# A fused decoder on one NeuronCore: rotary tables made by products and kept in DRAM, and an earlier timetable for keys and queries

## The chip, the cores and the metric

The kernel runs on one core of a Trainium2 chip. The core has a matrix engine (TensorE, PE in the profile; its weight loads are PEld), a vector engine (VectorE, DVE), a scalar engine with function tables (ScalarE, ACT), a general engine (GpSimd, POOL), and SyncE (SP), which here only issues DMA transfers. Each engine works off its own queue in order, and the engines wait for each other through semaphores. Data lie in DRAM, in SBUF (128 partitions) and in PSUM, where matmuls leave their results. The metric is the device time of one execution in microseconds (us); less is better.

## The reference

The program is a two-layer decoder over four batches of 256 tokens with 256 features. It runs six stages one after the other: rotary self-attention, attention to a masked memory, a ternary feed-forward, a convolution with a recurrence, attention of the tokens to a context of 1601 vectors and to themselves, and a mixture of eight experts of which each token takes two. The change lies in the last two. Cut to these, with the norms that come before them:

```python
x = x + xattn(_layernorm(x), ctx_2048, ...)          # 4 batches, 16 query heads, 4 key heads, 128 wide
x = x + experts(_layernorm(x), ...)

def _rope(x, pos):
    freqs = pos[:, None, :, None] * (1.0 / 10000.0 ** (arange(0, 128, 2) / 128))
    emb = concatenate((freqs, freqs), axis=-1)
    x1, x2 = split(x, 2, axis=-1)
    return x * cos(emb) + concatenate((-x2, x1), axis=-1) * sin(emb)

q = _rope(_rms_norm(tokens @ Wq.T, q_norm_w), token_positions)
kv_in = concatenate([context, tokens], axis=1)       # 1601 + 256 = 1857 keys
k = _rope(_rms_norm(kv_in @ Wk.T, k_norm_w), all_positions)
v = kv_in @ Wv.T                                     # k, v: each head serves four query heads
out = softmax(q @ k.T / sqrt(128)) @ v @ Wo.T

top_logits, top_idx = top_k(xf @ w_gate, 2)
weights = softmax(top_logits)
```

A key or query head of 128 values has two halves of 64. Rotation multiplies both by cosines, and adds the other half times sines. The norm's weights (`q_norm_w`, `k_norm_w`) can be multiplied into the cosines and sines, and the norm's scale, one number for a token or key and head, can be applied later.

## The kernel before

The first four stages of all batches take about the first 505 us. After that comes the part that the change touches: a loop over 32 pairs of query heads (two pairs to each of 16 heads (b, g), batch b and key head g), with the experts of batches 0 to 2 strewn in, until about 1700 us; the last batch's experts end the program.

**One pair** (class `Pair`). The queries of two heads and all 256 tokens are the 512 columns of each score matmul. The 1857 keys, tokens first, are 15 chunks of 128 (NCH); a pair has eight steps of two chunks (the last step has one). A step's `score` does, for each chunk, the matmul bsc (L1361), a copy on ACT that scales by the keys' norm kn (L1362), and on VectorE the running maximum acc (L1364, L1366). After the eighth step `maximum` transposes acc on TensorE (tm, L1373), VectorE reduces (mq, L1375), and TensorE spreads the result over the partitions (bc, L1379, in a PSUM bank of its own). Ten steps after its score, each step's `exponential` subtracts bc (L1383, VectorE), takes the exponential (L1386, ACT), and adds into the softmax's sum on POOL (L1389, L1398; fifteen sums for a pair). Eleven steps after its score, `weigh` multiplies by the values (bpo, L1407). So the second pair of a head scores while the first is weighed. `finish` divides by the sum and multiplies by Wo (bpw, L1437).

**What a head needs before its first score.** `prep_q(b, g, j)` makes the queries of one group of 128 tokens: two matmuls pq (L1239), the rotation (`rotate`: a square on ACT for the norm, L1189, and two products on VectorE with the tables ctab and stab, L1190 and L1191), then `factor`: an addition on POOL (ropeq, L1196), a reduction on VectorE (ssq, L1198), and a power on POOL (rnq, L1199). After a `yield`, ACT scales the four heads by rnq (`normed`, L1203). After another, TensorE transposes them (tpq, L1251) and ACT copies them to qT. `prep_kv(b, g, i)` does the same for unit i of up to four key chunks (pk, L1290); the power gives kn, which the score's copy applies later, and after one `yield` come the transposes tpk (L1301) and the copy to kT (L1303). Context keys and values of the last batch and part of the values of others are projected in advance and kept in DRAM (`kept_keys`, `kept_values`); `prep_kv` loads such raw keys, and `tiles` such values, by DMA on SP.

**Tables.** `angles(b)` makes, a piece at a time, cosines and sines for the 15 chunks' positions. `tables(b)` multiplies them by the norm's weights: four products for the keys (15 x 64 elements a partition each, L1160, L1161, L1164, L1165) and four small ones for the queries. A table has, for each chunk, 128 values in a row: the first half's 64, then the second's.

**The order.** The functions are generators. `steps` runs the loop; each step has two places, and `others(place)` advances the generators that `put` has set down for that place in the dictionary `places`. The timetable is relative to `base`, the place of the head before's first step, so a head's own scores begin at base + 32:

```python
QA, KA, HB, HC = (2, 6), (11, 13, 15, 17), 5, 8      # in steps for QA and KA, in places for HB and HC
DE, DW = 10, 11                                      # exponential and weighing come so many steps after a score
```

So the two query groups start at base + 4 and + 12, are scaled five places later, and transposed eight places after their start; key units 0 to 3 start at base + 22, 26, 30 and 34. A batch's first head also has its tokens' norm (-8, -6, -3), its query tables (-5, -3) and its key tables (+7, +11) there. `experts(b)` of an earlier batch goes in 23 pieces. A scheduler then orders each engine's queue from dependencies, so the order in the queues is not exactly that of the places. PSUM is a ring of six banks shared by all `p1` tiles, one bank for bc and one for the weighing's sum.

**Inverse roots.** `rsqrt` takes one instruction on VectorE and a power on POOL (L266 to 273); `newton` is eleven short ones on VectorE, with no POOL (L275 to 287). The norm ahead of attention (`normed_tokens`) and the one ahead of the experts (`experts`) use `rsqrt`.

**Routing.** In `experts` the two best logits' difference w2 is subtracted on VectorE and ACT's exponential of it (L1026) is issued in the same piece as the two maxima.

Of the kernel before, what the change touches and what calls it, by code (L numbers as in the profile page):

```python
# [20 lines left out]
P = 128  # L21
# [95 lines left out]
def decoder_kernel(ctx: ExitStack, tc: tile.TileContext, at, t, out):  # L117
# [861 lines left out]
    def experts(b):  # L979
# [10 lines left out]
        iota = cc("iota8")[:, None, :].to_broadcast(s8)  # L990
        mv = moments(xb, f"mo{b}")
        yield
        r1 = rsqrt(mv[:, :, 1], 1e-5, f"mo{b}")
        yield
        xh = centred(ea(f"mxh{b}"), xb, mv, r1)
        yield
# [26 lines left out]
            hots.append(oh)  # L1023
        w2 = sm([P, 2], "w2", f"w2{b}", 1)
        V.tensor_sub(w2, tops[1], tops[0])
        A.activation(w2, w2, AF.Exp)  # L1026
        yield
        w1 = sm([P, 2], "w1", f"w1{b}", 1)
# [86 lines left out]
    def angles(b):  # L1115
# [29 lines left out]
        d["angles"] = (ang, sn)  # L1145
        yield

    def tables(b, only="kq"):

        d = bt[b]  # L1150
        ang, sn = d["angles"]
        for nm, n, w in (("k", NCH, knw), ("q", 2, qnw)):
            if nm not in only:
                continue
            tb = [P, n, 64]
            ctab = wk.tile([P, n, HD1], F32, tag=f"c{nm}", name=f"ctab{nm}{b}")
            stab = wk.tile([P, n, HD1], F32, tag=f"s{nm}", name=f"stab{nm}{b}")
            wlo, whi = w[:, None, 0:64].to_broadcast(tb), w[:, None, 64:128].to_broadcast(tb)
            d[nm] = (ctab, stab)
            V.tensor_mul(ctab[:, :, 0:64], ang[:, 0:n, :], wlo)  # L1160
            V.tensor_mul(ctab[:, :, 64:128], ang[:, 0:n, :], whi)  # L1161
            yield

            V.scalar_tensor_tensor(stab[:, :, 64:128], sn[:, 0:n, :], -1.0, whi, ALU.mult, ALU.mult)  # L1164
            V.tensor_mul(stab[:, :, 0:64], sn[:, 0:n, :], wlo)  # L1165
            yield

    def normed_tokens(b):
        mv = moments(xs[b], f"xb{b}")
        r1 = rsqrt(mv[:, :, 1], 1e-5, f"xb{b}")  # L1170
        bt[b]["centred"] = lambda: centred(fa(0, f"bxh{b}"), xs[b], mv, r1)

    def token_features(b):
# [12 lines left out]
    def rotate(src, ctab, stab, sq, r, u):  # L1186


        A.activation(sq[:, :, 0:HD1], src, AF.Square)  # L1189
        V.tensor_mul(r, src, ctab)  # L1190
        V.tensor_mul(u, src, stab)  # L1191

    def factor(sq, r, u, n, nm, rn):

# [10 lines left out]
    def tiles(b, g):  # L1205

        if (b, g) not in gt:
            gt[b, g] = {

                "kT": odd("w3", f"kTb{b}{g}") if g % 2 else wk.tile([P, NKEY], F32, tag="kT", name=f"kTb{b}{g}"),  # L1210
                "v": (
                    odd("w4", f"vb{b}{g}")[:, 0 : NCH * HD1] if g % 2 else wk.tile([P, NCH * HD1], F32, tag="v", name=f"vb{b}{g}")
                ).rearrange("p (c d) -> p c d", c=NCH),
                "kn": sm([P, NCH], f"kn{g % 2}", f"kn{b}{g}", 1),
                "wkv": weight(
                    wk.tile([P, 512], F32, tag="wkv", name=f"wkv{b}{g}", bufs=2), "wkv1", 0, D, g * 256, (g + 1) * 256
                ),
            }
            for i in range(4):
                if (b, i) in kept_values:  # L1220
                    n, w = units(i)
                    r = min(P, w)
                    nc.sync.dma_start(
                        out=gt[b, g]["v"][0:r, 4 * i + 2 : 4 * i + 2 + n, :],
                        in_=kept_values[b, i][:, 0:r, g * HD1 : (g + 1) * HD1].rearrange("c p n -> p c n"),
                    )
        return gt[b, g]

    def prep_q(b, g, j):
        d, e = bt[b], tiles(b, g)  # L1230
        if j == 0:
            e["wq"] = weight(
                fb(0, f"wq{b}{g}"), "wq1", 0, D, g * 512, (g + 1) * 512
            )
            e["qT"] = fb(0, f"qTb{b}{g}").rearrange("p (h t) -> p h t", h=4)
        nm = f"q{b}{g}{j}"
        pq = p1(f"p{nm}")
        for c in range(2):
            T.matmul(pq, lhsT=d["yT"][:, c, j * P : (j + 1) * P], rhs=e["wq"][:, c, :], start=c == 0, stop=c == 1)  # L1239
        ctab, stab = (a[:, j : j + 1, :].to_broadcast([P, 4, HD1]) for a in d["q"])  # L1240

        rn = sm([P, 4], "rn4", f"rn{nm}", 4)
        sq, r, u = rope_tiles(nm)
        rotate(pq.rearrange("p (h d) -> p h d", h=4), ctab, stab, sq, r, u)
        factor(sq, r, u, 4, nm, rn)
        yield
        normed(r, rn, 4)
        yield
        tp = p1(f"tp{nm}")
        for h in range(4):  # L1250
            T.transpose(tp[:, h * P : (h + 1) * P], r[:, h, :], ident)  # L1251
        A.copy(e["qT"][:, :, j * P : (j + 1) * P], tp.rearrange("p (h t) -> p h t", h=4))
# [5 lines left out]
    def prep_kv(b, g, i):  # L1258

        d, e = bt[b], tiles(b, g)  # L1260
        nm = f"k{b}{g}{i}"
        n = min(4, NCH - 4 * i)
        k0 = max(0, 4 * i - 2)
        w = (4 * i + n - 2 - k0) * P
        done = 0
        if b in kept_keys:
            done = n if i else 2
            raw = db(f"raw{nm}")[:, 0 : done * HD1].rearrange("p (c d) -> p c d", c=done)
            nc.sync.dma_start(
                out=raw, in_=kept_keys[b][k0 : k0 + done, :, g * HD1 : (g + 1) * HD1].rearrange("c p n -> p c n")  # L1270
            )
        else:
            cT = db(f"cT{nm}")[:, 0 : 2 * w].rearrange("p (c n) -> p c n", c=2)
            nc.sync.dma_start(out=cT, in_=t["ctxT"][b][:, k0 * P : k0 * P + w].rearrange("(c p) n -> p c n", p=P))
        sq, r, u = rope_tiles(nm)
        if done:
            o = n - done
            ctab, stab = (a[:, 4 * i + o : 4 * i + n, :] for a in d["k"])
            rotate(raw, ctab, stab, *(a[:, o:n, :] for a in (sq, r, u)))
        for h in range(0, n - done, 2):  # L1280
            m = min(2, n - h)
            pk = p1(f"p{nm}{h}").rearrange("p (c n) -> p c n", c=2)
            there = [k >= 2 and (b, (k - 2) // 4) in kept_values for k in range(4 * i + h, 4 * i + h + m)]
            for q in range(m):
                k = 4 * i + h + q
                w = HD1 if there[q] else 2 * HD1
                for c in range(2):
                    o = (k - 2 - k0) * P
                    src = d["yT"][:, c, k * P : (k + 1) * P] if k < 2 else cT[:, c, o : o + P]
                    T.matmul(pk[:, q, 0:w], lhsT=src, rhs=e["wkv"][:, c, 0:w], start=c == 0, stop=c == 1)  # L1290
            ctab, stab = (a[:, 4 * i + h : 4 * i + h + m, :] for a in d["k"])
            rotate(pk[:, 0:m, 0:HD1], ctab, stab, *(a[:, h : h + m, :] for a in (sq, r, u)))
            assert len(set(there)) == 1
            if not there[0]:
                A.copy(e["v"][:, 4 * i + h : 4 * i + h + m, :], pk[:, 0:m, HD1:256])

        factor(sq, r, u, n, nm, e["kn"][:, 4 * i : 4 * i + n])
        yield
        tp = p1(f"tp{nm}")
        for q in range(n):  # L1300
            T.transpose(tp[:, q * P : (q + 1) * P], r[:, q, :], ident)  # L1301
        w = min(512, NKEY - 512 * i)
        A.copy(e["kT"][:, 512 * i : 512 * i + w], tp[:, 0:w])  # L1303

    def before_head(b, g):

        if g == 0:
            if b == 0:
                yield from angles(b)
            yield from tables(b)  # L1310
        late = None
        for i in (1, 2, 3):
            gen = prep_kv(b, g, i)
# [138 lines left out]

    QA, KA, HB, HC = (2, 6), (11, 13, 15, 17), 5, 8
    DE, DW = 10, 11
    places, taken = {}, set()
    STEPS = NPAIR * len(pairs) + DW + 5
# [34 lines left out]
    for k, (b, g) in enumerate(heads):  # L1493
        base = 32 * (k - 1)
        if k:
            if g == 0:
                gen = angles(b)
                for i in range(9):
                    put(base - 81 + 6 * i, gen, i == 8)
                gen = tokens(b)  # L1500
                for i, o in enumerate((-8, -6, -3)):
                    put(base + o, gen, i == 2, i == 2)
                for o, n in ((-5, "q"), (-3, "q"), (7, "k"), (11, "k")):
                    gen = tables(b, n) if o in (-5, 7) else gen
                    put(base + o, gen, o in (-3, 11))
            for f, when in ((prep_q, QA), (prep_kv, KA)):
                for i, o in enumerate(when):
                    gen = f(b, g, i)
                    spot = put(base + 2 * o, gen, bank=f is prep_q)
                    if f is prep_q:  # L1510
                        put(spot + HB, gen)
                    put(spot + HC, gen, True, True)
        gen = loader(b, g)
        put(base + 60, gen, True)
    for b in range(B - 1):
        gen = experts(b)
        spot = 2 * (64 * (b + 1) + 17)

        pieces = 23 if b < B - 2 else 23 - 2 * KEPT
        for i in range(pieces):  # L1520
            spot = put(spot, gen, i == 22, i not in (0, 1, 2, 5, 6)) + (5 if i > 6 else 3)
    kept = gen

    def others(place):
# [145 lines left out]
```

## Time and profile before

| | |
|---|---|
| three runs before | 1749.51, 1746.26, 1751.23 us; median 1749.51 |
| the profiled execution's own time | 1749.43 us |
| its span in the trace | 1747.4 us |
| mean granted TensorE clock | 0.993 |
| instructions in the trace | 20643 |
| DMA traffic | 119.10 MB, mean 68 GB/s |

The page follows the work that ended last back through the program: 64% of the span is on PE, 12% on DVE, 9% each on POOL and ACT, 4% is issue and 1% DMA. Of lines, the weighing bpo (L1407) has 17%, the scores bsc (L1361) 16%, and the key projections pk (L1290) and POOL's sums (L1398) 5% each.

The costliest groups, with their count and the mean time of one:

| engine, line | what | count | mean of one |
|---|---|---|---|
| PE L1361 | scores bsc, 512 columns | 960 | 599 ns |
| PE L1407 | weighing bpo, 512 columns | 960 | 598 ns |
| ACT L1362 | copy of scores | 480 | 683 ns |
| DVE L1366 | running maximum | 448 | 743 ns |
| DVE L1383 | scores less maximum, 2 x 512 | 256 | 1142 ns |
| ACT L1386 | exponential, 2 x 512 | 256 | 1006 ns |
| POOL L1398 | softmax's sum, 512 | 411 | 1306 ns |
| ACT L1203 | scaling of the queries | 128 | 390 ns |

How to read this: a matmul of 128x512 is listed as x4 because the compiler cuts float32 matmuls into four passes; 480 score tiles are thus 960 listed here in two forms (counts in the trace are of instructions as the profiler saw them). The share of busy time is a mean over a program of two very different parts. The first 505 us and the pair loop have other limits, so the stretches of the loop have to be read by themselves. An idle engine costs time only if it is the one that the end waits for; here the question is what PE waits for inside the loop, and for how long.

### The profile page before, as it was taken

The numbers are of one execution on the slowest core, as the hardware profiler recorded it, in microseconds if no ns is written. First come the engines' busy times: TensorE is split into PE (matmuls) and PEld (weight loads), VectorE is DVE, ScalarE is ACT, GpSimd is POOL, SyncE is SP. The second block draws the span as 40 slices with busy tenths as digits, with TensorE's granted clock in tenths as the row PEclk, the third lists the DMA queues.
The fourth block names the chain that finished last, engine by engine and source line by source line (L and its number), as shares of the span: only waits on it lengthen the run. The fifth ranks groups of instructions, "written<-read, shape, count | busy, mean of one in ns | idle before, by whom it ended". The sixth has DMA issues, their size and how long they took to land.

```text
span 1747.4 us, 20643 instructions
## 1 busy us (share of the span) xinstructions
PE 1694.9 (97%) x6642; PEld 971.5 (56%) x6642; DVE 1302.7 (75%) x2429; ACT 997.4 (57%) x1742; POOL 877.5 (50%) x719
## 2 busy tenths in 40 slices
PE   8899989999999999999999999999999999999998
PEld 4455668765555455554555555555555555445546
DVE  6653476787668777787877878777877878788776
ACT  3456653656456656566665656556565656656551
POOL 2210032211126576676766756655665776676651
PEclk9999999999999999999999999999999999999999
DMA  7221334212231121121212121121222113011102
GB/s 258 99 90 50 90 99 128 75 66 90 97 109 46 38 82 35 55 58 31 89 32 70 47 67 52 55 82 35 73 61 67 51 37 93 26 37 48 43 0 67
DMA packets 113554, 119.10 MB, mean 68 GB/s; under 512 B 10000, under 2 KB 87332, under 8 KB 113448
## 3 DMA queue, kind: packets, MB, share of 16 engines
q1 hardware_dynamic: 111624, 116.39, 21.6%
q10 hardware_dynamic: 1824, 1.41, 0.3%
q8 instruction: 53, 0.87, 0.2%
q14 instruction: 53, 0.43, 0.1%
HBM read 100.20 MB, written 17.57 MB: 67 GB/s over the span
## 4 chain that ended last, share of the span: by engine, by line
PE 64%; DVE 12%; POOL 9%; ACT 9%; issue 4%; DMA 1%; POOLq 0%; DVEq 0%; ACTq 0%
PE bpo L1407 17%; PE bsc L1361 16%; PE pk L1290 5%; POOL sum L1398 5%; PE mph L1053 2%; PE bpw L1437 2%; PE vah L355 2%; ACT s L1386 2%; ACT s L1362 2%; DVE acc L1366 1%; PE xpo L740 1%; DVE s L1383 1%; PE pq L1239 1%; POOL ropeq L1196 1%; PE xsc L695 1%
## 5 line engine op out<-in xcount | busy, mean ns | idle before, releaser
L1398 POOL TENSOR_TENSOR sum<-sum,s 128x512 f32<-128x512 f32 (+1 forms) x411 | 536.7, 1306 | 84.1 <-ACT s L1386 59.0
L1361 PE MATMUL bsc<-qTb,kTb 128*128 128x512 f32 (+1 forms) x960 | 459.5, 599 | 6.8 <-ACT kTb L1303 6.7
L1407 PE MATMUL bpo<-s,vb 128*128 128x512 f32 (+1 forms) x960 | 459.9, 598 | 0.4 <-ACT s L1386 0.4
L1362 ACT ACTIVATE s<-bsc,kn 128x512 f32<-128x512 f32 (+1 forms) x480 | 316.5, 683 | 211.6 <-PE bsc L1361 194.6
L1366 DVE SCALAR_TENSOR_TENSOR acc<-bsc,kn,acc 128x512 f32<-128x512 f32 x448 | 333.0, 743 | 89.2 <-ACT s L1362 73.3
L1383 DVE TENSOR_TENSOR s<-s,bc 128x1024 f32<-128x1024 f32 (+1 forms) x256 | 289.4, 1142 | 14.7 <-PE bc L1379 14.5
L1386 ACT ACTIVATE s<-s 128x1024 f32<-128x1024 f32 (+1 forms) x256 | 256.5, 1006 | 53.8 <-DVE s L1383 52.2
L1361 PEld LDWEIGHTS bsc<-qTb,kTb 128*128 128x128 f32 (+1 forms) x960 | 174.2, 188 | 191.9 <-issue 135.3
L1407 PEld LDWEIGHTS bpo<-s,vb 128*128 128x128 f32 (+1 forms) x960 | 169.8, 191 | 141.7 <-issue 137.9
L1389 POOL TENSOR_TENSOR sum<-s 128x512 f32<-128x512 f32 x32 | 40.8, 1276 | 198.6 <-ACT s L1386 198.6
L1196 POOL TENSOR_TENSOR ropek<-ropek,ropuk 128x512 f32<-128x512 f32 (+1 forms) x64 | 78.2, 1222 | 123.7 <-DVE ropuk L1191 122.4
L1203 ACT ACTIVATE ropeq<-ropeq,rnq 128x128 f32<-128x128 f32 x128 | 41.2, 390 | 110.7 <-POOL rnq L1199 107.1
L355 PE MATMUL vah<-wv,vcT 128*128 128x512 f32 (+1 forms) x156 | 77.7, 633 | 5.1 <-DMA vcT<-in_ctxT 3.1
L1290 PEld LDWEIGHTS pk<-wkv,cTk 128*128 128x128 f32 x624 | 76.3, 192 | 8.3 <-issue 4.5
L1290 PE MATMUL pk<-wkv,cTk 128*128 128x128 f32 x624 | 77.4, 275 | 0.0
L1199 POOL TENSOR_TENSOR kn<-ssk,nhalf 128x4 f32<-128x4 f32 (+1 forms) x64 | 66.2, 1034 | 17.5 <-DVE ssk L1198 15.0
L1364 DVE TENSOR_SCALAR acc<-bsc,kn 128x512 f32<-128x512 f32 x32 | 24.0, 750 | 59.7 <-ACT s L1362 59.7
L1437 PEld LDWEIGHTS bpw<-wo,aT 128*128 128x128 f32 x256 | 48.5, 190 | 34.8 <-issue 21.1
L272 POOL TENSOR_TENSOR rsr_xa<-rse_xa,nhalf 128x2 f32<-128x2 f32 x4 | 3.4, 854 | 126.0 <-DVE rse_xa L270 126.0
L1437 PE MATMUL bpw<-wo,aT 128*128 128x256 f32 x256 | 65.6, 379 | 0.3 <-ACT aT L1413 0.3
L1196 POOL TENSOR_TENSOR ropeq<-ropeq,ropuq 128x512 f32<-128x512 f32 x32 | 43.8, 1368 | 40.2 <-PE bsc L1361 17.8
L358 ACT COPY vst<-vah 128x512 f32<-128x512 f32 (+1 forms) x52 | 30.2, 591 | 56.0 <-issue 18.3
(509 smaller groups left out, 2589.7 us busy)
## 6 DMA issues: line engine op xcount, KB each, us to landing
v<-vst SPq DMA_DIRECT2D x48, 256.0 KB
vb<-v SPq DMA_DIRECT2D x48, 256.0 KB
cTk<-in_ctxT SPq DMA_DIRECT2D x24, 512.0 KB
wq<-in_wq SPq DMA_DIRECT2D x16, 512.0 KB
wo<-in_wo SPq DMA_DIRECT2D x16, 512.0 KB
wi<-in_wi SPq DMA_DIRECT2D x32, 256.0 KB
xcT<-in_ctxT SPq DMA_DIRECT2D x12, 512.0 KB
xct<-in_ctx SPq DMA_DIRECT2D x12, 512.0 KB
```

The lines of the kernel that those rows point to most:

```text
L355: T.matmul(pv[0:r, :], lhsT=cT[:, c, k * P : k * P + r], rhs=wv[c], start=c == 0, stop=c == 1)
L1196: G.tensor_tensor(r4, r4, u4[:, :, ::-1, :], ALU.add)
L1199: G.tensor_tensor(rn, ss[:, 0:n], nhalf[:, 0:n], ALU.pow)
L1290: T.matmul(pk[:, q, 0:w], lhsT=src, rhs=e["wkv"][:, c, 0:w], start=c == 0, stop=c == 1)
L1361: T.matmul(pc[0:n, :], lhsT=e["kT"][:, k * P : k * P + n], rhs=q, start=True, stop=True)
L1362: A.activation(s[0:n, i, :], pc[0:n, :], AF.Copy, scale=e["kn"][0:n, k : k + 1])
L1366: V.scalar_tensor_tensor(self.acc[0:n, :], pc[0:n, :], e["kn"][0:n, k : k + 1], self.acc[0:n, :], ALU.mult, ALU.max)
L1383: V.tensor_tensor(s[0:n, 0:w, :], s[0:n, 0:w, :], self.bc[0:n, None, :].to_broadcast([n, w, 512]), ALU.subtract)
L1386: A.activation(s[0:n, 0:w, :], s[0:n, 0:w, :], AF.Exp)
L1398: G.tensor_tensor(self.sum[0:n, :], self.sum[0:n, :], s[0:n, i, :], ALU.add)
L1407: T.matmul(self.po, lhsT=e["v"][0:n, k, :], rhs=self.s[c][0:n, i, :], start=k == 0, stop=k == NCH - 1)
L1437: T.matmul(pw[:, j * 256 : j * 256 + 256], lhsT=aT[:, o : o + P], rhs=e["wo"][:, self.h + h, :], start=True, stop=True)
```

## The change

**Tables by halves, one product at a time.** `tables` is taken apart. `new_tables` allots the cosine and sine tables with the half as the outer index, [P, 2, n, 64] in place of [P, n, 128], and `quarter` makes one of the four products. `rotate` and its callers read the tables through four-dimensional views. For batches 1 to 3 the four key products go, each by itself, into a scratch tile and by DMA to DRAM (`tables_ahead`, at places base - 29, -24, -19, -14), and `load_tables` fetches them into the tables at base + 3. The query tables are made at base - 7 and -4. Batch 0 makes its tables in place, as before.

**Timetable.** Query groups start at base + 1 and + 7 (were + 4 and + 12), are scaled nine places later (was five) and transposed twelve places after their start (was eight). Key units start in the order 1, 2, 0, 3 at base + 14, 18, 23 and 27 (were 0, 1, 2, 3 at + 22, 26, 30, 34), with their transposes still eight places later. Kept values are loaded by a generator of their own at base + 22, in place of inside `tiles`.

**Roots.** `normed_tokens` for batches 1 to 3 and `experts` for batches 0 to 2 take their inverse roots by `newton`, through a new function `root`.

**Routing.** A `yield` stands between the subtraction and the exponential, so `experts` has one piece more.

```diff
-        r1 = rsqrt(mv[:, :, 1], 1e-5, f"mo{b}")
+        r1 = rsqrt(mv[:, :, 1], 1e-5, f"mo{b}") if final else root(mv, f"mo{b}")
...
         V.tensor_sub(w2, tops[1], tops[0])
+        yield
         A.activation(w2, w2, AF.Exp)
...
+    def new_tables(b, nm):
+        n = NCH if nm == "k" else 2
+        bt[b][nm] = tuple(wk.tile([P, 2, n, 64], F32, tag=f"{c}{nm}", name=f"{c}tab{nm}{b}") for c in "cs")
+        return bt[b][nm]
+
+    def quarter(b, nm, i, dst):
+        n, w = (NCH, knw) if nm == "k" else (2, qnw)
+        src = bt[b]["angles"][i // 2][:, 0:n, :]
+        k = 1 - i % 2 if i > 1 else i % 2
+        w = w[:, None, 64 * k : 64 * k + 64].to_broadcast([P, n, 64])
+        if i == 3:
+            V.tensor_mul(dst, src, w)
+        elif i == 2:
+            V.scalar_tensor_tensor(dst, src, -1.0, w, ALU.mult, ALU.mult)
+        else:
+            V.tensor_mul(dst, src, w)
+
     def tables(b, only="kq"):
-        ...
-            V.tensor_mul(ctab[:, :, 0:64], ang[:, 0:n, :], wlo)
-            V.tensor_mul(ctab[:, :, 64:128], ang[:, 0:n, :], whi)
-            yield
-            V.scalar_tensor_tensor(stab[:, :, 64:128], sn[:, 0:n, :], -1.0, whi, ALU.mult, ALU.mult)
-            V.tensor_mul(stab[:, :, 0:64], sn[:, 0:n, :], wlo)
-            yield
+        for nm in only:
+            tabs = new_tables(b, nm)
+            for i in range(4):
+                quarter(b, nm, i, tabs[i // 2][:, (1 - i % 2) if i > 1 else i % 2])
+                if i % 2:
+                    yield
+
+    def tables_ahead(b):
+        kept_tables[b] = []
+        for i in range(4):
+            w = db(f"tab{b}{i}")[:, 0 : NCH * 64]
+            quarter(b, "k", i, w.rearrange("p (n d) -> p n d", n=NCH))
+            d = dram.tile([P, NCH * 64], F32, tag=f"t{b}{i}", name=f"t{b}{i}")
+            nc.sync.dma_start(out=d, in_=w)
+            kept_tables[b].append(d)
+            yield
+
+    def load_tables(b):
+        tabs = new_tables(b, "k")
+        for i, d in enumerate(kept_tables[b]):
+            nc.sync.dma_start(
+                out=tabs[i // 2][:, (1 - i % 2) if i > 1 else i % 2].rearrange("p n d -> p (n d)"), in_=d
+            )
+        yield
+
+    def root(mv, nm):
+        v = sm([P, 2], "rse2", f"rse_{nm}")
+        V.tensor_scalar(v, mv[:, :, 1], 1e-5, None, ALU.add)
+        return newton(v, nm, 2)
...
     def normed_tokens(b):
-        r1 = rsqrt(mv[:, :, 1], 1e-5, f"xb{b}")
+        r1 = root(mv, f"xb{b}") if b else rsqrt(mv[:, :, 1], 1e-5, f"xb{b}")
...
     def rotate(src, ctab, stab, sq, r, u):
         A.activation(sq[:, :, 0:HD1], src, AF.Square)
-        V.tensor_mul(r, src, ctab)
-        V.tensor_mul(u, src, stab)
+        src4, r4, u4 = (a.rearrange("p n (h d) -> p n h d", h=2) for a in (src, r, u))
+        V.tensor_mul(r4, src4, ctab)
+        V.tensor_mul(u4, src4, stab)
...
-    QA, KA, HB, HC = (2, 6), (11, 13, 15, 17), 5, 8
+    QA, KA, HB, HC, HQ = (1, 7), ((1, 14), (2, 18), (0, 23), (3, 27)), 9, 8, 12
...
             if g == 0:
+                gen = tokens(b)
+                for i, o in enumerate((-8, -6, -3)):
+                    put(base + o, gen, i == 2, i == 2)
                 gen = angles(b)
                 for i in range(9):
                     put(base - 81 + 6 * i, gen, i == 8)
-                gen = tokens(b)
-                for i, o in enumerate((-8, -6, -3)):
-                    put(base + o, gen, i == 2, i == 2)
-                for o, n in ((-5, "q"), (-3, "q"), (7, "k"), (11, "k")):
-                    gen = tables(b, n) if o in (-5, 7) else gen
-                    put(base + o, gen, o in (-3, 11))
-            for f, when in ((prep_q, QA), (prep_kv, KA)):
-                for i, o in enumerate(when):
-                    gen = f(b, g, i)
-                    spot = put(base + 2 * o, gen, bank=f is prep_q)
-                    if f is prep_q:
-                        put(spot + HB, gen)
-                    put(spot + HC, gen, True, True)
+                gen = tables_ahead(b)
+                for i in range(4):
+                    put(base - 29 + 5 * i, gen, i == 3)
+                gen = tables(b, "q")
+                for i in range(2):
+                    put(base - 7 + 3 * i, gen, i == 1)
+                put(base + 3, load_tables(b), True)
+            for i, o in enumerate(QA):
+                gen = prep_q(b, g, i)
+                spot = put(base + o, gen, bank=True)
+                put(spot + HB, gen)
+                put(spot + HQ, gen, True, True)
+            for i, o in KA:
+                gen = prep_kv(b, g, i)
+                put(base + o, gen)
+                put(base + o + HC, gen, True, True)
+            put(base + 22, load_values(b, g), True)
...
-        pieces = 23 if b < B - 2 else 23 - 2 * KEPT
+        pieces = 24 if b < B - 2 else 24 - 2 * KEPT
```

## The prediction

> **What bounds the kernel now.** First the page's busy times, then stretches of 100 us (columns: stretch, length, then busy us of PE, PEld, DVE, ACT, POOL, the granted clock, DMA share and GB/s).
> ```profile
> PE 1694.9 (97%) x6642; PEld 971.5 (56%) x6642; DVE 1302.7 (75%) x2429; ACT 997.4 (57%) x1742; POOL 877.5 (50%) x719
> ```
> ```profile
> 600.00:700.00 100.00, 99.24 (x364) 53.55 (x363) 78.20 (x126) 63.48 (x108) 65.88 (x55) 1.00 0.18 54
> 700.00:800.00 100.00, 96.86 (x351) 51.78 (x350) 81.85 (x124) 60.08 (x97) 65.31 (x50) 0.98 0.21 63
> 1000.00:1100.00 100.00, 97.06 (x357) 54.90 (x356) 80.49 (x127) 55.06 (x90) 62.54 (x48) 0.98 0.21 64
> 1500.00:1600.00 100.00, 96.04 (x309) 49.96 (x309) 81.33 (x139) 58.79 (x99) 66.54 (x52) 0.98 0.12 33
> ```
> TensorE is the bound, at full clock. The change leaves every matmul in place, so it can win only PE's idle time. From 500 to 1700 us the twelve stretches leave 19.9 us, half of it in the three shown last. Next, what PE waits for after 500 us (total us, times, longest), and ACT's largest wait on POOL from 505 to 1700 us.
> ```profile
> PE bc L1379 <- DVE mq L1375: 6.9, 3, 2.5
> PE bsc L1361 <- ACT kTb L1303: 6.7, 10, 1.2
> PE tpk L1301 <- DVE it L1060: 3.0, 5, 0.7
> PE tm L1373 <- DVE acc L1366: 2.3, 1, 2.3
> ```
> ```profile
> ACT ropeq L1203 <- POOL rnq L1199: 105.9, 30, 6.5
> ```
> The timeline around one such wait shows the chain.
> ```profile
> 739.44 9.15 POOL L1398 TENSOR_TENSOR sum<-sum,s 128x512 f32<-128x512 f32 x6 [0.53 <-ACT s L1386]
> 749.77 1.01 POOL L1199 TENSOR_TENSOR rnq<-ssq,nhalf 128x4 f32<-128x4 f32 x1
> 750.82 1.28 ACT L1203 ACTIVATE ropeq<-ropeq,rnq 128x128 f32<-128x128 f32 x4 [6.07 <-POOL rnq L1199]
> 752.70 0.75 DVE L1364 TENSOR_SCALAR acc<-bsc,kn 128x512 f32<-128x512 f32 x1 [5.23 <-ACT s L1362]
> 753.37 0.68 DVE L1375 TENSOR_REDUCE mq<-tm 128x4 f32<-128x512 f32 x1
> 754.10 0.65 PE L1379 MATMUL bc<-cst,mq 128*128 128x128 f32 x4 [2.26 <-DVE mq L1375]
> 754.59 2.97 PE L1361 MATMUL bsc<-qTb,kTb 128*128 128x512 f32 x4
> ```
> POOL sums come first, so the queries' power (rnq) is late. ACT's scaling of the queries (L1203) stands in its queue and blocks the score copies behind it. VectorE's first maximum waits for those, mq stands behind it, and PE waits for mq. Four score matmuls then take 2.97 us instead of 1.88, so the listed waits understate the loss. I took every matmul's start and subtracted the pace of the one before (four of 512 columns start every 1.72 us). After 505 us that loses 30.3 us: three bc places with the slow matmuls behind them 4.1, 4.1 and 2.3; the tm place (1550 us) 4.1; nine places where a score waits for the last quarter of kT, 7.7; five tpk places 3.8; the rest 4.2, of which 2.3 lie in the tail, untouched.
>
> **The change part by part.** The profiled execution took 1749.43 us (span 1747.4), as good as the median 1749.51; sums start there. Distances below are PE work at the pace above, counted in the two programs' orders of instructions.
>
> *Queries.* The same instructions (two matmuls, a square, two products, a reduction, a POOL addition and power, four scalings, four transposes) stand earlier: projections 74 to 80 and 60 to 67 us before the head's first score, against 64 to 71 and 43 to 49. In POOL's queue the first group's addition and power (1.37 and 1.11 us) now stand ahead of a pair's sums, and the second's behind nine of the fifteen (9 x 1.31 = 11.8 us after the first). But ACT's scaling still stands only a few instructions behind the square. I work out an ACT wait of about 1.5 us for the first group (0.59 + 0.68 + 0.68 + 1.37 + 1.11 = 4.4 less about 3 of work between) and about 4 for the second: 15 x 5.5 = 82 us, not nothing. What changes is what it hits: the bc of a head's first pair lies 30 to 35 us before that score, and the second wait used to fall just there; now it falls some 20 us sooner, in mid-pair, with at least 3.4 us of PE work between uses of one PSUM buffer. Gain 0 to 10.5; I take 10.5. The tpk waits come from the same ACT wait (a tanh behind it): 0 to 3.8, I take half, 1.9.
>
> *Keys.* Units run 1, 2, 0, 3, at 48 to 11 us ahead of the first score. The last unit's transpose stood 24 to 27 us after that score and its reader 27 to 30, hence 7.7 us; it now stands 9 to 11 after, the reader 25 to 29. I take 7.0. Unit 0's transpose stays 1.7 to 2.6 us ahead, covered by a 0.86 us weighing matmul against a 0.59 us copy: 0. The tm place has raw keys' products ahead of the last maximum on VectorE; they move, and I take 2.0 of 4.1. For the last batch, unit 3's raw load waits for unit 2's product and is used 3.4 us of PE work later in three heads: 0 to 1 us each, I take 1.0 in all.
>
> *Tables.* For three batches four products move ahead, and 12 stores and 12 loads of 492 KB are added, all on SP. Their prices and a plain neighbour:
> ```profile
> L1161 DVE TENSOR_TENSOR ctabk<-ang,knw 128x960 f32<-128x960 f32 x4 | 6.7, 1666 | 0.0
> L1160 DVE TENSOR_TENSOR ctabk<-ang,knw 128x960 f32<-128x960 f32 x4 | 6.5, 1622 | 0.0
> L1131 DVE TENSOR_TENSOR ang<-pf,cst 128x960 f32<-128x960 f32 x4 | 4.6, 1145 | 0.0
> ```
> With 1.44 and 1.46 for the other two that is 6.2 us a batch, moved and not added. The first three (4.7 us) now stand within three steps, between a rotation and a pair's last maximum, and tm waits for that maximum: 0 to 4.7 a batch; I take 1.0, 3.0 in all. Each store makes SP wait for VectorE, with the next head's context, wi and wq loads behind it. They are used at least 20 us of PE work after the last thing SP waits for, the tables 34 or more, and 2 x 1.97 MB at 284 GB/s (the best slice from 1330 to 1440 us) is 13.8 us: 0. Without that cover a projection would wait out the rest.
>
> The Trainium skill (SBUF — State Buffer, Who interferes with whom) says a VectorE tensor_tensor with two SBUF inputs and a GpSimd instruction reading SBUF lock each other out for a whole instruction. The trace agrees: these products took 1.78 and 1.83 us at 716.75 and 724.49, and a scalar_tensor_tensor of the same size took 1.15 at 733.12. By that rule each moved product could cost one sum (1.31 us) more, 12 x 1.31 = 15.7, and the forecast would be about 1749.
>
> *Roots.* Six powers on POOL (0.70 each) become Newton steps: 11 more VectorE instructions of about 0.17 (L270's rows: 164 and 171 ns), 6 x 11 x 0.17 = 11.2 us. VectorE's waits for these powers (4.0 and 1.6 us) go. The net 5.6 hides in its 20% idle; 0 to 5.6, I take 1.0.
>
> *The rest.* Values are loaded later, past the point where SP was held for them: 0; weighing starts over 50 us after the load's place. Routing's exponential apart from its maximum: no ACT wait on it is listed: 0. Rotations read tables in runs of 64: POOL's addition in such runs (L1196, 1293 ns) costs no more than a plain sum (1308): 0; the upper bound is in the third rival.
>
> *Sum.* 10.5 + 1.9 + 7.0 + 2.0 = 21.4 won; 1.0 + 3.0 + 1.0 = 5.0 paid. 1749.4 - 16.4 = **1733.0 us**; own range 1724 to 1745.
>
> **The rivals.** *All of it goes.* All four groups (26.1 us), nothing paid: 1723.3. For it, one cause feeds most of them; against it, ACT still waits some 80 us.
>
> *The waits only move.* ACT's scaling blocks elsewhere and PE loses the same 16 us at other places; only the last quarter of kT is won: 1749.4 - 7.0 + 5.0 = 1747. For it, 30 ACT waits exist and only three hit bc; against it, mid-pair waits now cost PE under 1 us each.
>
> *Slower: rotation in halves.* All rotation products (L1190, L1191: 145 us in all) now read 64-element runs. If that costs what separates L1160 from L1131 (1622 against 1145, x 1.43), VectorE gets 62 us more over fifteen heads. It decides once VectorE passes some 90% of a head from 80; half would land on PE: 1733 + 31 = 1764. Against it: L1131 itself reads runs of 64 and is the fast one, and L1164 wrote such runs at 1.15 us.
>
> **How the numbers follow.** Forecast 0.59, all of it 0.14, moved 0.15, slower 0.12. Below 1744.2 (0.3%, what a measurement can tell) lie nearly all of the first, the second and a quarter of the third: faster 0.75; same 0.13; slower 0.12. The range 1722 to 1752 takes in both neighbours and leaves the slow case out.
>
> **What would show it.** Right: bc waits under 2 us in all; kTb waits under 2; ACT still waiting 50 to 100 us for rnq; PE busy over 98% from 700 to 1600; no PE wait on a DMA. Wrong: PE waits on tm near the products tab (VectorE full), L1190 above 480 ns for 128x256 (halves), or a pk matmul waiting for cT (SP held).

## The result, and the profile after

The changed kernel takes 1770.92 us (median of 1768.68, 1770.62, 1771.23 and 1772.16) against 1749.41 us before: 1.0123 times, 95% interval 1.0106 to 1.0141. It is slower by 21.5 us, where 16.4 us less were forecast; the time lies above the range. The profiled execution took 1768.68 us with a span of 1766.8, 19.4 us above that of before. Of all the runs below, one (of both query groups ahead of the sums) took 2198.82 us at a granted clock of 0.752; its ratio is made of the other four.

The page's busy times, and the stretches that answer to those shown of before (columns as there):

```profile
PE 1698.2 (96%) x6642; PEld 971.0 (55%) x6642; DVE 1304.8 (74%) x2495; ACT 996.3 (56%) x1742; POOL 871.7 (49%) x713
```
```profile
600.00:700.00 100.00, 93.86 (x344) 50.51 (x344) 85.97 (x129) 56.73 (x97) 65.63 (x51) 1.00 0.24 76
700.00:800.00 100.00, 99.07 (x364) 53.61 (x363) 74.35 (x121) 64.46 (x104) 67.83 (x56) 1.00 0.25 80
1000.00:1100.00 100.00, 97.27 (x371) 55.60 (x370) 77.75 (x126) 65.12 (x104) 67.59 (x57) 1.00 0.27 85
1500.00:1600.00 100.00, 93.98 (x303) 47.23 (x302) 76.19 (x127) 58.12 (x99) 66.43 (x53) 1.00 0.13 37
```

TensorE has the same 6642 matmuls, VectorE 66 instructions and 2.1 us more; TensorE idles longer. From the first matmul's start to the last one's it takes 1741.5 us before and 1761.2 us after, and these 19.7 us are the whole loss of the two profiled executions. Next, what PE waits for after 505 us (total us, times, longest), and ACT's wait for the queries' powers.

```profile
PE bpo L1450 <- ACT aT L1456: 10.2, 11, 2.6
PE bsc L1404 <- DVE acc L1409: 6.4, 9, 1.1
PE tm L1416 <- DVE acc L1409: 4.6, 5, 1.7
PE bpw L1480 <- DVE acc L1409: 4.6, 9, 0.7
PE tpq L1293 <- DVE acc L1409: 2.8, 3, 0.9
PE bc L1422 <- DVE mq L1418: 1.5, 2, 1.3
```
```profile
ACT ropeq L1241 <- POOL rnq L1237: 127.8, 30, 7.5
```

The old waits went: bc from 6.9 to 1.5 us, kT's copy from 6.7 and tpk from 3.0 us to no row at all. New ones took their place and are larger: the copy of the weighed sum (aT) and the running maximum in mid-pair. ACT's wait for rnq (the queries' power) did not fall to 82 us but rose from 105.9 to 127.8. The timeline of an early head shows one such wait and what it does (start, duration, engine and line, what it does, and in brackets the idle time before it and what ended that):

```profile
581.30 10.73 POOL L1441 TENSOR_TENSOR sum<-sum,s 128x512 f32<-128x512 f32 x8 [0.79 <-ACT s L1429]
...
585.51 1.29 ACT L1405 ACTIVATE s<-bsc,kn 128x512 f32<-128x512 f32 x2
...
585.93 0.68 DVE L1236 TENSOR_REDUCE ssq<-squares 128x4 f32<-128x516 f32 x1
...
593.22 1.01 POOL L1237 TENSOR_TENSOR rnq<-ssq,nhalf 128x4 f32<-128x4 f32 x1
...
594.26 1.28 ACT L1241 ACTIVATE ropeq<-ropeq,rnq 128x128 f32<-128x128 f32 x4 [7.46 <-POOL rnq L1237]
...
596.15 0.75 DVE L1409 SCALAR_TENSOR_TENSOR acc<-bsc,kn,acc 128x512 f32<-128x512 f32 x1 [6.82 <-ACT s L1405]
...
596.95 1.07 PE L1404 MATMUL bsc<-qTb,kTb 128*65 128x512 f32 x2 [0.84 <-DVE acc L1409]
...
598.74 1.13 PE L1480 MATMUL bpw<-wo,aT 128*128 128x256 f32 x4 [0.72 <-DVE acc L1409]
```

The second query group's sum of squares is ready at 586.6 us. Its power stands behind eight sums (10.73 us) and an addition on POOL and ends at 594.2. ACT's scaling stands at the head of ACT's queue all that time: ACT does nothing for 7.46 us, the score copies behind it are late, VectorE's maximum with them, the PSUM ring fills, and TensorE waits twice. In fourteen of the fifteen heads that are prepared in the loop ACT waits some 2 us for the first group's power and 5.0 to 7.5 for the second's. In the 15 us behind these fourteen longer waits TensorE idles 20 us in all, from nothing to 3.3 us a head.

The largest waits for aT (1.5 us at 697 us, 2.2 at 1005, 2.6 at 1549) fall 26 to 32 us behind such a wait of ACT, at a change of pair, where ACT is itself waiting for VectorE's subtraction. When only the scaling is held (below), the waits at these places are 0.7, 0.4 and 1.0 us, so most of them follows from it; the way there was not traced.

The section on time and profile before gives four passes of the compiler as the reason for an x4. No row shows that: the rows have two matmuls to a score tile, 960 for 480, and an x4 of the timeline is two such tiles.

### The profile page after: what moved, and what is told of

Its sections match the earlier page's. It is cut to its first block, busy times and chain, and to the rows that moved or that the text cites. A ratio compares the mean times of both kernels' runs of the same rounds, so it can differ in the third digit from the quotient of the medians.

```text
span 1766.8 us, 20705 instructions
## 1 busy us (share of the span) xinstructions
PE 1698.2 (96%) x6642; PEld 971.0 (55%) x6642; DVE 1304.8 (74%) x2495; ACT 996.3 (56%) x1742; POOL 871.7 (49%) x713
## 5 line engine op out<-in xcount | busy, mean ns | idle before, releaser
L1450 PE MATMUL bpo<-s,vb 128*128 128x512 f32 (+1 forms) x960 | 459.9, 597 | 10.6 <-ACT aT L1456 10.2
L1484 DVE SCALAR_TENSOR_TENSOR x<-bpw,rs,x 128x256 f32<-128x256 f32 x128 | 55.5, 473 | 11.1 <-PE bpw L1480 11.1
```

Source lines behind the costliest of these rows:

```text
L1450: T.matmul(self.po, lhsT=e["v"][0:n, k, :], rhs=self.s[c][0:n, i, :], start=k == 0, stop=k == NCH - 1)
```

## The experiments

Each time is a median of four to six runs, beside runs of the kernel before on the same chip (1749.23 us in the first four, 1747.29 in the next four, 1746.72 in the last).

**The queries' places put back.**

```diff
-    QA, KA, HB, HC, HQ = (1, 7), ((1, 14), (2, 18), (0, 23), (3, 27)), 9, 8, 12
+    QA, KA, HB, HC, HQ = (4, 12), ((1, 14), (2, 18), (0, 23), (3, 27)), 5, 8, 8
```


> The changed kernel with the queries' places of before (groups at +4 and +12, scaled 5 and transposed 8 places after). Theory Q (the second group's power stands behind nine sums of a pair in POOL's queue, ACT's scaling waits up to 7.5 us for it in mid-pair, and about 22 of the 46 us of late matmul starts follow from that): the mid-pair losses go, about 10 us of the old waits for bc come back, 1771 - 22 + 10 = 1759 us. Theories T (tables) and K (keys): the queries are not at fault, 1771 us within 3.

1733.49 us, 0.9914 (0.9899 to 0.9928). The queries' places alone turn a gain of 16 us into a loss of 21. ACT's wait for rnq is 85.2 us, its longest 4.7. The effect is 37 us where I had worked out 12: waits that I had put down to the batch changes went too.

**The keys' order put back.**

```diff
-    QA, KA, HB, HC, HQ = (1, 7), ((1, 14), (2, 18), (0, 23), (3, 27)), 9, 8, 12
+    QA, KA, HB, HC, HQ = (1, 7), ((0, 22), (1, 26), (2, 30), (3, 34)), 9, 8, 12
```


> The changed kernel with the keys' order and places of before (units 0 to 3 at +22, 26, 30, 34). Theory K (the new places put the keys' rotation where VectorE has a pair's last maximum, which is the waits of tm and of the first weighing, about 10 us in the last batch's heads and 10 elsewhere): 1771 - 15 + 8 for kT's last quarter = 1764 us. Theories Q and T: only kT's last quarter comes back, 1771 + 8 = 1779 us.

1808.18 us, 1.0334 (1.0314 to 1.0354), worse than either theory said. The row and the timeline tell why:

```profile
PE bsc L1404 <- ACT kTb L1345: 57.8, 14, 6.5
```
```profile
587.88 0.49 PE L1343 MATMUL tpk<-cst,ropek 128*128 128x128 f32 x3
...
592.83 1.01 POOL L1237 TENSOR_TENSOR rnq<-ssq,nhalf 128x4 f32<-128x4 f32 x1
...
593.88 0.69 ACT L1241 ACTIVATE ropeq<-ropeq,rnq 128x128 f32<-128x128 f32 x2 [7.26 <-POOL rnq L1237]
...
595.91 0.42 ACT L1345 COPY kTb<-tpk 128x321 f32<-128x321 f32 x1
596.38 3.40 PE L1404 MATMUL bsc<-qTb,kTb 128*128 128x512 f32 x4 [5.43 <-ACT kTb L1345]
```

The transposes of the last key quarter ended at 588.4 us; their copy stood in ACT's queue behind the same scaling for rnq until 595.9. In the same head of the changed kernel ACT's wait of 7.46 us was followed by 1.6 us of idle TensorE; here 7.26 us cost it 5.4 at once, because an instruction that TensorE needs next stands behind the scaling.

**The tables put back, and the roots and routing put back**, each by itself in the changed kernel.

```diff
-                gen = tables_ahead(b)
...
-                put(base + 3, load_tables(b), True)
+                for o, n in ((-5, "q"), (-3, "q"), (7, "k"), (11, "k")):
+                    gen = tables(b, n) if o in (-5, 7) else gen
+                    put(base + o, gen, o in (-3, 11))
```


> The changed kernel with the key tables made in place at +7 and +11 and the query tables at -5 and -3, as before, still laid out by halves; no stores and loads of tables. Theory T (with the key products gone ahead, the angles' tiles come free at the batch change and the next batch's nine angle instructions, some 9 us of VectorE, fall there, beside the last maximum and the keys' rotation): the losses of 4.9, 3.1 and 1.8 us at the three batch changes go, 1771 - 9 = 1762 us. Theories Q and K: 1771 us within 3.

1769.07 us, 1.0115 (1.0098 to 1.0132), against 1.0123 for the changed kernel: by the ratios 1.4 us less, which can't be told from nothing.

```diff
-        r1 = rsqrt(mv[:, :, 1], 1e-5, f"mo{b}") if final else root(mv, f"mo{b}")
+        r1 = rsqrt(mv[:, :, 1], 1e-5, f"mo{b}")
...
-        r1 = root(mv, f"xb{b}") if b else rsqrt(mv[:, :, 1], 1e-5, f"xb{b}")
+        r1 = rsqrt(mv[:, :, 1], 1e-5, f"xb{b}")
...
         V.tensor_sub(w2, tops[1], tops[0])
-        yield
         A.activation(w2, w2, AF.Exp)
```


> The changed kernel with the inverse roots on POOL and routing's exponential in one piece with the maxima, as before. Theories Q, T and K: 1771 us within 3, since the six roots' 66 short VectorE instructions (11 us) lie in its idle time. If the roots are at fault, 1762 to 1766 us.

1771.75 us, 1.0136 (1.0118 to 1.0153): no effect that can be told. (The edit also takes back the one piece that `experts` had more.)

**The scaling held.** This tells the place of the queries from the place of the scaling in ACT's queue. An ordering edge without a semaphore keeps the scaling behind the ACT instructions that the program issues before it.

```diff
+        held = latest()
         normed(r, rn, 4)
+        if (b, g) != (0, 0):
+            keep_behind(held)
         yield
...
-    QA, KA, HB, HC, HQ = (1, 7), ((1, 14), (2, 18), (0, 23), (3, 27)), 9, 8, 12
+    QA, KA, HB, HC, HQ = (1, 7), ((1, 14), (2, 18), (0, 23), (3, 27)), 13, 8, 16
```


> The changed kernel, with only ACT's scaling of the queries bound behind the ACT instructions that the program issues before it, and placed 13 instead of 9 places after the group's start (transposes 16 instead of 12). On POOL the second group's power still stands behind eight or nine sums. Theory W (not the power's place costs the time, but the scaling that stands at the head of ACT's queue meanwhile, with the score copies, the copy of the weighed sum and kT's copy behind it): ACT's wait for rnq falls from 127.8 to under 20 us, and the time to 1733 us within 8. Rival P (the queries' earlier places as such, their PSUM banks and VectorE products, cost the 37 us that the queries' old places won back): 1771 us within 5, whatever ACT waits.

1729.88 us, 0.9899 (0.9885 to 0.9914): some 40 us less than the changed kernel, with the second group's power on POOL still behind eight or nine sums of a pair. After 505 us ACT has no row of its scaling waiting for rnq any more, and from its first start to its last TensorE takes 1722.1 us, 39.1 less than in the changed kernel. The longest in total of PE's waits are now:

```profile
PE bpo L1453 <- ACT aT L1459: 2.5, 4, 1.0
PE tpq L1296 <- ACT ropeq L1241: 1.9, 2, 1.0
```

The earlier places cost nothing by themselves that can be told (0.9899, against 0.9900 for the keys alone further down); rival P falls.

**Both groups ahead of the sums.**

```diff
-    QA, KA, HB, HC, HQ = (1, 7), ((1, 14), (2, 18), (0, 23), (3, 27)), 9, 8, 12
+    QA, KA, HB, HC, HQ = (0, 2), ((1, 14), (2, 18), (0, 23), (3, 27)), 6, 8, 12
```


> The changed kernel with both query groups started at +0 and +2 and scaled six places later; both groups' additions and powers then stand ahead of a pair's first sum in POOL's queue. Theory W: ACT waits for two powers with no sum ahead of them, at most 2 x 2.5 us a head, 1733 us within 6. Rival P (earlier places cost): both groups are earlier still, 1771 us or more.

1785.16 us, 1.0214 (1.0199 to 1.0228): a miss. ACT's waits for rnq did become short, and the time grew all the same:

```profile
ACT ropeq L1241 <- POOL rnq L1237: 76.2, 30, 3.1
```
```profile
PE bpo L1450 <- ACT aT L1456: 42.6, 17, 3.2
```
```profile
583.67 1.02 POOL L1237 TENSOR_TENSOR rnq<-ssq,nhalf 128x4 f32<-128x4 f32 x1
584.72 0.69 ACT L1241 ACTIVATE ropeq<-ropeq,rnq 128x128 f32<-128x128 f32 x2 [3.14 <-POOL rnq L1237]
...
587.41 0.58 ACT L1456 COPY aT<-bpo 128x512 f32<-128x512 f32 x1
...
588.04 3.54 PE L1450 MATMUL bpo<-s,vb 128*128 128x512 f32 x4 [2.74 <-ACT aT L1456]
```

Here the wait falls at a change of pair. The last weighing has ended at 583.6 us; the copy that frees its single PSUM bank stands behind the scaling and three other instructions, and the next pair's first weighing waits for it in nearly every head. So theory W was too wide: the sum of ACT's waits does not set the cost; what stands behind the waiting instruction does.

**The same with the scaling held**, by the same ordering edge as above, to test that narrower form:

```diff
-    QA, KA, HB, HC, HQ = (0, 2), ((1, 14), (2, 18), (0, 23), (3, 27)), 6, 8, 12
+    QA, KA, HB, HC, HQ = (0, 2), ((1, 14), (2, 18), (0, 23), (3, 27)), 13, 8, 16
```


> The queries' places +0 and +2 that gave 1785 us, with ACT's scaling bound behind the ACT instructions that the program issues before it, and placed 13 instead of 6 places after the group's start (transposes 16 instead of 12). The powers on POOL stay where they were, ahead of a pair's first sum. Theory W in its narrower form (the length of ACT's wait does not count but what stands behind it: there the copy of the weighed sum, aT, for which the next pair's first weighing waits with a single PSUM bank): PE's waits for aT fall from 42.6 to under 6 us, and the time to 1731 us within 6. Rival P (so early places cost by themselves, through banks or VectorE): above 1765 us.

1730.38 us, 0.9906 (0.9892 to 0.9921), with 6.3 us of waits for aT and 3.8 us of ACT waiting for rnq. Some 54 us come back with the queries' matmuls and the powers at the same places.

**The second group late.**

```diff
-    QA, KA, HB, HC, HQ = (1, 7), ((1, 14), (2, 18), (0, 23), (3, 27)), 9, 8, 12
+    QA, KA, HB, HC, HQ = (1, 15), ((1, 14), (2, 18), (0, 23), (3, 27)), 5, 8, 8
```


> The changed kernel with the second query group moved from +7 to +15, scaled five and transposed eight places after a group's start; its power then stands behind all sums of a pair, and the first group's ahead of the next pair's. Theory W: the second wait is that of before at a pair's end (2 to 5 us) while POOL is nearly done, 1736 us within 8. Rival P: half of the old places are back, about 1752 us.

1731.03 us, 0.9908 (0.9893 to 0.9923). With the second power behind all of a pair's sums but also requested late, ACT waits 52.9 us in all, 2.6 at the longest.

**The keys alone**, in the kernel before, with the queries as they were there.

```diff
-    QA, KA, HB, HC = (2, 6), (11, 13, 15, 17), 5, 8
+    QA, KA, HB, HC = (2, 6), ((1, 14), (2, 18), (0, 23), (3, 27)), 5, 8
...
+            for i, o in KA:
+                gen = prep_kv(b, g, i)
+                put(base + o, gen)
+                put(base + o + HC, gen, True, True)
```


> The kernel before with only the keys' new order and places. The prediction's term (kT's last quarter 7.0 us, and the wait of tm 2.0): 1749 - 9 = 1740 us. Theory S (the whole gain over before that the changed kernel has with the queries put back, 16 us, is from the keys): 1733 us. Theory T (the tables bring half of it): 1741 us.

1730.02 us, 0.9900 (0.9885 to 0.9915): 17.3 us from the keys alone, all that the changed kernel without its queries' places has over before. The rest of the change brings nothing that can be told.

**Queries and tables both put back** (the first and third edits together).

> The changed kernel with both the queries' places and the tables put back; the keys' order, the halves, the roots and routing's exponential stay. Theory T (the tables made ahead cost the waits of tm at the batch changes, 4.1 us, which is why the run with the queries alone put back was 3 us slower than the keys alone): 1729 us. Theory N (the tables neither cost nor bring anything that can be measured): 1733 us within 2.

1731.56 us, 0.9911 (0.9896 to 0.9926), between the two expectations. By the ratios that is 0.5 us less than with the queries alone put back: here too the tables neither cost nor bring anything that can be told.

**The scaling held in the kernel before**, first with the keys' new order and then without it; the edit shown is the one without it.

```diff
+        held = latest()
         normed(r, rn, 4)
+        if (b, g) != (0, 0):
+            keep_behind(held)
...
-    QA, KA, HB, HC = (2, 6), (11, 13, 15, 17), 5, 8
+    QA, KA, HB, HC = (2, 6), (11, 13, 15, 17), 8, 8
...
-                    put(spot + HC, gen, True, True)
+                    put(spot + HC + 3 * (f is prep_q), gen, True, True)
```


> The kernel before with the keys' new order and ACT's scaling of the queries bound as in the other runs of this kind, scaled 8 and transposed 11 places after the group's start (were 5 and 8). Theory W: the waits of bsc, tm, tpk and bpo that the keys alone leave, some 8 us, are mostly behind the same scaling, 1725 us within 3. Rival F (nothing of the rest is due to it): 1730 us.

1732.53 us, 0.9914 (0.9899 to 0.9929): nothing more than the keys alone. Rival F holds for this pair.

> The kernel before with only ACT's scaling of the queries bound and placed later (8 and 11 places). The prediction's reading (bc and tpk wait for the scaling, 10.5 + 3.8 us; kT's last quarter, 7.7 us, waits because its places are late): 1747 - 14 = 1733 us. Theory W to its end (kT's copy, too, stood behind the scaling): 1725 us. If the scaling was not the cause of before's waits: 1747 us.

1725.45 us, 0.9873 (0.9857 to 0.9890), the fastest of all kernels here, 21 us below before and some 44 below the changed kernel by the ratios, with none of the change in it. The longest in total of PE's waits after 505 us:

```profile
PE bc L1382 <- DVE mq L1378: 2.4, 1, 2.4
PE mpe L1066 <- DVE it L1060: 1.4, 1, 1.4
PE bpo L1410 <- ACT aT L1416: 0.8, 1, 0.8
PE bsc L1364 <- ACT kTb L1306: 0.6, 2, 0.4
```

The waits for kT's copy fell from 6.7 to 0.6 us though the keys kept their old, late places. From its first start to its last TensorE takes 1718.1 us here, 23 less than before, and 1724.5 with the keys' new order as well, where it waits 2.9 us in tm and 2.5 for aT; why the new order costs these once nothing blocks ACT stays open. In none of the held runs was the edge separated from the places by which the scaling and the transposes were moved later.

## Why the prediction was wrong, point by point

**What bounds the kernel** held. TensorE was the bound, its work did not change, and the chain from POOL's sums over rnq and ACT's scaling to the score copies was read rightly.

**The queries' step failed, and it is the one that set the sign.** It worked out a wait of ACT of "about 1.5 us for the first group" and "about 4 for the second", and that in mid-pair nothing would come of it, since there is "at least 3.4 us of PE work between uses of one PSUM buffer". The runs showed 2 us and 5.0 to 7.5 us. The prediction had counted the nine sums (11.8 us) ahead of the second power, but its 4 us left most of them out of the wait. At 7 us the slack of the ring is gone: TensorE idles up to 3.3 us a head in mid-pair, and the waits for aT that the step did not have add 10.2 us in all. The gain of 12.4 us that the step names (bc and tpk) mostly came (bc fell to 1.5 us, tpk to no row); its price, put at nothing, was larger. Putting the queries back wins 37 us, and holding the scaling alone, with the queries where they are, some 40.

**The keys' step named the wrong cause.** It took kT's wait for late places, "hence 7.7 us". The kernel before's own timeline shows the transposes done in time and the copy behind the scaling:

```profile
583.73 1.28 ACT L1203 ACTIVATE ropeq<-ropeq,rnq 128x128 f32<-128x128 f32 x4 [4.04 <-POOL rnq L1199]
...
585.74 0.49 PE L1301 MATMUL tpk<-cst,ropek 128*128 128x128 f32 x3
...
589.09 0.43 ACT L1303 COPY kTb<-tpk 128x321 f32<-128x321 f32 x1
...
589.57 1.98 PE L1361 MATMUL bsc<-qTb,kTb 128*128 128x512 f32 x4 [0.76 <-ACT kTb L1303]
```

The copy starts 2.9 us after its transposes end (585.74 + 0.49), since ACT has 4 us to make up. Holding the scaling took this wait away without moving a key. The keys' new order also brought more than the 9.0 us in the sum, 17.3: in that run neither kT's copy nor bc has a row any more, and ACT's wait for rnq is 83.0 us, its longest 4.5, where it was 105.9 and 6.5. That the keys' work, moved out from behind the scaling, brings all of this is argued and not shown.

**Tables**: 3.0 us was the price taken; the two runs showed 1.4 and 0.5, no more than nothing and far from the 15.7 us of twelve blocked sums. After 505 us PE has no wait on a DMA, so the stores and loads, and the last batch's raw loads (1.0 in the sum), show no cost there. The prediction also read the products' rows too simply. At 357 to 367 us, where no sum runs on POOL, all four take 1.15 us; beside POOL's sums and additions of the later batches they take 1.55 to 1.91, but for the scalar_tensor_tensor at 733.12 us: it took 1.15, and the sum beside it 2.07 in place of 1.27. So both kinds of product collide, and what differs is which engine is held up.

**Roots**, 1.0, and **routing**, 0: no effect that can be told, 1.0136 without them against 1.0123. **Rotation in halves**, 0, held, and the slower rival's mechanism falls: its 1764 us came nearest to the measured time by luck, and its factor (1622 against 1145 is 1.42, not 1.43) was made by these collisions and not by the layout. These are the products' rows (count, then shortest, median and longest in ns), against medians of 416 and 681 before:

```profile
L1228 DVE TENSOR_TENSOR ropek<-pk,ctabk x100: 275/414/425, 403.0 to 1630.2; 128x256 f32<-128x256 f32 x88, 128x128 f32<-128x128 f32 x12
L1228 DVE TENSOR_TENSOR ropeq<-pq,ctabq x32: 669/691/693, 478.5 to 1589.3; 128x512 f32<-128x512 f32 x32
```

**The rivals.** The right kind was "The waits only move": ACT's scaling blocks elsewhere. Its price was wrong: it let PE lose the same 16 us at other places, and against it stood that a wait in mid-pair costs under 1 us. That sentence should have been turned round, and the case carried past the old time: with ACT's wait growing, nothing bounds the new loss by the old one. The time of 1733 us that was forecast is what the change takes with its queries put back, but by other terms than those of the sum.

## What to carry to other kernels

Where an instruction waits at the head of an engine's queue, list what stands behind it up to the next thing that the bounding engine needs; its cost is read there, and neither from the length of the wait nor from how early the work itself is started. When a producer is moved into a busy queue (here a power behind eight sums), add the queue ahead of it to the wait before calling it hidden. And before moving work, try to move only the instruction that waits: holding one scaling back won more than the whole timetable.

## What was not expected of the hardware

A long wait of TensorE can be paid twice. In the run with both groups first, the matmuls after a wait of 2.74 us show a granted clock of 0.60, and four score-sized ones take 3.54 us in place of 1.88 to 1.98:

```profile
585.00:588.00 3.00, 0.30 (x1) 0.00 (x0) 2.13 (x4) 3.00 (x7) 0.99 (x1) 0.97 0.00 0
588.00:592.00 4.00, 3.96 (x6) 1.85 (x7) 4.00 (x5) 3.62 (x6) 3.05 (x4) 0.60 0.02 4
592.00:596.00 4.00, 4.00 (x18) 1.61 (x17) 2.41 (x6) 3.15 (x4) 3.76 (x4) 1.00 0.00 2
```

In that run TensorE started late by 2.7 to 3.3 us, against the pace that the prediction uses, in 14 places, and in 9 of them the matmuls behind lost another 1.4 to 1.8 us at half pace. With the keys put back, 12 of 14 late starts of 2.8 to 6.7 us cost another 1.4 to 3.1. In the changed kernel the two latest starts after 505 us (2.3 and 2.8 us) had none of it, and its mean clock was 0.996.

The Trainium skill (TensorE: Matmul & The Clock Gate, What's actually happening) says that the clock halves after an idle window of about 3.4 us that runs free of the program. These runs agree that the same wait is sometimes followed by half pace and sometimes not; that waits of 2.4 to 3.3 us, shorter than that window, can already be enough is what the traces add (in the kernel before, three of the four starts late by 2.3 to 2.6 us lost another 1.3 to 1.6).
